# Masked self-attention with a residual: small count groups move from a shared buffer pool to spare columns of the context's bank, and one pair's turn of reciprocals changes place

## The chip, the cores and the metric

The kernel runs on one core of a Trainium2 chip. The time is device microseconds of one execution, the median of several. The figures in the profile come from one further execution that was recorded by the profiler. PE is the matrix engine, DVE the vector engine, ACT the scalar engine, POOL and SP the engines that issue most DMA transfers. PSUM is the memory that PE writes to; it has eight banks of 512 single floats per partition.

## The reference

`x` is (16, 512, 1024), batch by channel by token; `mask` is (16, 1024) of zeros and ones, about half of them ones; both weights are (512, 512).

```python
xt = jnp.transpose(x, (0, 2, 1))
q = xt @ Wq.T                                    # one projection for Q, K and V
qh = q.reshape(B, T, 8, 64).transpose(0, 2, 1, 3)
scores = scale * jnp.einsum('bhqd,bhkd->bhqk', qh, qh)
logits = (scores * cmask + (1.0 - cmask) * NEG) * rmask
attn = jax.nn.softmax(logits, axis=-1)
ctx = jnp.einsum('bhqk,bhkd->bhqd', attn, qh)
out = ctx.transpose(0, 2, 1, 3).reshape(B, T, D) @ Wo.T
return x + jnp.transpose(out, (0, 2, 1))
```

A token with mask 0 is no key, and as a query it attends to all tokens alike, so its context is the mean. Only the tokens with mask 1 need scores.

## The kernel before

**Tiling.** The sixteen batches are sorted by their number of active tokens and worked one after the other. The active tokens of a batch are gathered by indirect DMA (POOL), and up to 544 of them (528 or 512 in other batches) go through query, scores, softmax and context. The eight heads are worked as four pairs, p = 0 to 3. Each batch has 18 steps: four for each pair, and one more at 1 and at 10 for the tail tokens beyond 512.

**Who sets the order.** PE's order is written by hand: a table `plan` lists for each (step, half) which pieces of work stand there, and `free[step]` lists pieces that stand at the start of a step, ahead of its scores. Inside a batch PE does the scores of this batch (`scores`, L823), its contexts (`attend`, L858), the query projection of the next batch (`query`, L591, twelve matmuls for each half), the values (L654), and the product of the batch before with Wo (`project`, here `P_(i)`, L982, twelve matmuls, followed by the add of x on DVE, L988). The orders of DVE, ACT and SP are made by a scheduler from the program's order, ties and priorities; `high_priority(offset=HPO)` marks an instruction as urgent.

**PSUM.** `pm` hands out one of two single-bank buffers; whoever takes one waits until the reader of what stood in it is done. The other six banks are one tile, `ps` (named pss in the profile). Scores go to its banks 0 to 4 and are read there by the exps (`p<-pss`, ACT L838); the context goes to columns from 240 of banks 4 and 5. The first 240 columns of bank 5 are free, and `spot(n)` gives the first n of them. I call them the strip. All groups that use the strip use the same columns, so each waits for the reader of the group before it. Before the change the strip has four users: `index` (read by DVE at L372), `top` (L714, read by L717 into m), `bottom` (L727, read by L730 into nm) and the turn of pair 3.

**The turn.** `recip_sums` makes the reciprocal of each softmax row's sum in a column (ending in DVE L905). `recip_rows(b, p)`, the turn, transposes that column tile by one PE instruction (L912, 128x128), copies ten rows out (L917, rr), and sends them by SP to DRAM and back to all partitions (rd, rb), where `norm` multiplies the context with them (L964). Pairs 0, 1 and 2 turn in pm, pair 3 in the strip.

**Counts.** For a group of batches, `slots` works out where each active token goes: 16 matmuls with 2 to 32 columns (L254, L256, L259) give running counts `pr` and totals `pn`, read on DVE at L260, L262 and L266. It runs in batches b = 0, 2, 6, 9 and 12. `facts_end` (b = 1, 3, 7, 10 and 13) sums mask values by one matmul (L351) into `pe`, read at L352. Ahead of slots stand `permute` and `active` (DVE only), ahead of facts_end `facts_sums` (DVE only).

**Tail batches.** In b = 2, 5, 8, 11 and 14 a further product with Wo (`project_tail`) stands at step 10.

**Ties.** The framework orders accesses to one tile. `other_banks(i, ...)` declares that instruction i has nothing to do with others; `left` holds the exps in flight, `spot_reads` the reads of the strip that the next scores need not wait for.

Of the kernel before, what the change touches and what calls it, by code (L numbers as in the profile page):

```python
# [19 lines left out]
P = 128  # L20
# [27 lines left out]
class Fast:  # L48
# [12 lines left out]
    def __init__(self, ctx, tc, x, x_nat, mask_t, wq_t, wo_t, out):  # L61
        self.tc, self.nc = tc, tc.nc
        self.x, self.x_nat, self.out = x, x_nat, out
        self.B = B = x.shape[0] // T
        self.wide = [512 if b in (0, B - 2, B - 1) else C if b < 5 else 528 for b in range(B)]
        self.kept = [C if b < B - 2 else 512 for b in range(B)]
        pool = lambda name, bufs, **k: ctx.enter_context(tc.tile_pool(name=name, bufs=bufs, **k))
        self.const = pool("const", 1)
        self.one = pool("one", 1)
        self.dram = pool("dram", 8, space=bass.MemoryType.DRAM)  # L70
        self.ps_m = pool("ps_m", 2, space=PS)
        self.begun = ExitStack()
        self.ps_0 = self.begun.enter_context(tc.tile_pool(name="ps_0", bufs=2, space=PS))
        self.ps_w = self.begun.enter_context(tc.tile_pool(name="ps_w", bufs=1, space=PS))
        self.context_out, self.left, self.read, self.spots, self.spot_reads = None, [], [], False, []
# [168 lines left out]
    def slots(self, b0, b1):  # L244
# [7 lines left out]
        mb, mh = self.act  # L252
        pr = self.pm([P, B, TB])
        nc.tensor.matmul(pr, lhsT=self.tri, rhs=mh, start=True, stop=False)  # L254
        for s in range(1, TB):
            nc.tensor.matmul(pr[:, :, s:], lhsT=self.on16, rhs=mh[:, :, :TB - s], start=False, stop=(s == TB - 1))  # L256
        pn = self.pm([P, B])
        for j in range(TB):
            self.pe = nc.tensor.matmul(pn, lhsT=self.on16, rhs=mh[:, :, j], start=(j == 0), stop=(j == TB - 1)).ins  # L259
        nc.vector.tensor_copy(n, pn)  # L260
        base = self.sb([P, B, TB], F32, "sc", 3)
        nc.vector.tensor_tensor(base, self.tok.unsqueeze(1).broadcast_to([P, B, TB]), pr, ALU.subtract)  # L262
        nc.vector.tensor_tensor(base, base, n.unsqueeze(2).broadcast_to([P, B, TB]), ALU.add)
        slot = self.sb([P, NC], F32, "sc", 3)
        s3 = slot.rearrange("p (b j) -> p b j", j=TB)
        nc.vector.tensor_tensor(s3, pr, base, ALU.subtract)  # L266
        nc.vector.tensor_tensor(s3, s3, mb, ALU.mult)
# [77 lines left out]
    def facts_end(self, b0, b1):  # L345
        nc = self.nc
        B = b1 - b0
        ok = self.ok[:, b0:b1]
        t = self.sb([P, B], F32, "sc", 3)
        pe = self.pm([P, B])  # L350
        nc.tensor.matmul(pe, lhsT=self.on16, rhs=self.whole_masks, start=True, stop=True)  # L351
        nc.vector.tensor_scalar(t, pe, float(T), None, ALU.is_equal)  # L352
        nc.vector.tensor_tensor(ok, ok, t, ALU.mult)
# [9 lines left out]
    def index(self, b):  # L363
# [7 lines left out]
        base = self.base[:, b:b + 1]  # L371
        i = s["at"] = nc.vector.tensor_scalar(s["idx"], pi, base, None, ALU.add).ins  # L372
        self.spot_reads += [i] * self.spots
        with self.behind(i):
# [39 lines left out]
    def spotted(self, i):  # L414
        if self.spots:
            self.other_banks(i.ins, *self.left)
        return i

    def needs(self, i, *others):
# [290 lines left out]
    def top(self, b, g):  # L710
# [5 lines left out]
        with self.tc.high_priority(offset=HPO):  # L716
            i = nc.vector.tensor_reduce(m, pt, AX.X, ALU.max).ins  # L717
        if self.spots:
            self.other_banks(i, *self.left)
            self.spot_reads.append(i)  # L720

    def bottom(self, b, g):
# [6 lines left out]
        with self.tc.high_priority(offset=HPO):  # L729
            self.spot_reads += [nc.vector.tensor_scalar(nm[:, :HG], pb, -SCALE, None, ALU.mult).ins] * self.spots  # L730
        t = self.sb([P, HG], F32, "nq", 2)
# [56 lines left out]
    def scores(self, b, p, u):  # L788
# [46 lines left out]
        for j in (0, 1, 2, 3) if opening else (3, 0, 1, 2):  # L835
            k, i, at = places[j]
            t = self.sb([P, C], F32, "p", 12)[:, :A]
            e = nc.scalar.activation(t, flat[:, at:at + A], AF.Exp, bias=s["nm"][p // 2][:, p % 2 * 2 + k:p % 2 * 2 + k + 1],  # L838
                                     scale=SCALE, accum_out=s["z"][:, 2 * p + k, i:i + 1]).ins
            self.exp = [e]  # L840
            self.left.append(e)
# [3 lines left out]
    def attend(self, b, p, after=None):  # L845
# [18 lines left out]
        self.pend = b, p, pav, exps  # L864
        self.spot_reads = []

# [40 lines left out]
    def recip_rows(self, b, p):  # L907
# [8 lines left out]
        with self.tc.high_priority(offset=HPO):  # L916
            self.recip = nc.vector.tensor_copy(rr, pt[:10]).ins  # L917
            self.spot_reads += [self.recip] * spot
        rd = self.dram.tile([10, P], F32, tag="rd", name="rd")
# [174 lines left out]
    def run(self, flag):  # L1094
# [128 lines left out]
        if True:  # L1223
            stack = ExitStack()
            for b in range(B + 1):
# [21 lines left out]
                pk, tp, bt = ((lambda o, g, f=f, c=c: [(c, L(f, o, g))]) for f, c in ((self.peaks, 0), (self.top, 0.1), (self.bottom, 0.1)))  # L1247
                new = [g for g in groups if b == g[0] - 2], [g for g in groups if b == g[0] - 1]
                if n < B:
                    q, x, v = (lambda e, g: query(n, e, g)), xt(n), (lambda e: [(0.25, L(self.value, n, e))])  # L1250
# [7 lines left out]
                    if b:  # L1258
# [12 lines left out]
                    else:  # L1271
# [48 lines left out]
                for st, (p, i) in enumerate(S):  # L1320
# [173 lines left out]
```

## Time and profile before

| | |
|---|---|
| Time, median of 3 runs | 963.98 us (963.57 to 964.73) |
| Profiled execution, its own time | 965.21 us |
| Profiled execution, span | 963.5 us |
| PE clock granted | 0.999 of full speed |
| POOL busy | 305.1 us, 32% of the span |

The profile's page lists busy time by engine, the chain of waits that ended last, and the costliest groups. In a row of the timeline stand the start in us, the duration in us, the engine, the line, the operation, the tiles as output<-inputs, the shape, the count of instructions, and in brackets the idle time before it with what ended it. A row with a count above 1 covers that many instructions, one behind the other.

### The profile page before, as it was taken

What the parts mean: (1) busy time and instruction counts of PE and PEld (TensorE: products, weight loads), DVE (VectorE), ACT (ScalarE), POOL (GpSimd) and SP (SyncE); (2) the same over time, 40 slices, a digit from 0 to 9 for tenths busy, and PEclk for the clock granted to TensorE, in tenths of its full rate; (3) what the DMA queues carried; (4) which work ended last, traced back from release to release, by engine and by line L of the source; (5) the groups of instructions that cost most, each with busy time, mean ns of one, the idle gap of its engine ahead of it and who ended that gap; (6) DMA issues with size and microseconds to landing.
All of it is one profiled execution on the core that took longest, in us unless ns stands there. A gap on an engine that the chain in (4) does not pass through costs nothing.

```text
span 963.5 us, 22790 instructions
## 1 busy us (share of the span) xinstructions
PE 931.5 (97%) x8121; PEld 581.3 (60%) x8121; DVE 721.1 (75%) x2443; ACT 644.7 (67%) x1669; POOL 305.1 (32%) x311
## 2 busy tenths in 40 slices
PE   6799999999999999999999999999999999999997
PEld 4556656566666666666666566666666666565543
DVE  7779677776777767887678687877877788685563
ACT  4778766667677666776767678665767866665651
POOL 2102022142241513415144250522515135252452
PEclk9999999999999999999999999999999999999999
DMA  5756556556675666756656787654767757555552
GB/s 172 222 175 203 155 154 183 163 180 190 180 209 148 194 197 193 220 157 199 177 181 204 198 239 223 177 158 136 214 168 233 243 144 207 151 161 161 171 175 102
DMA packets 78568, 176.30 MB, mean 183 GB/s; under 512 B 14480, under 2 KB 22416, under 8 KB 78448
## 3 DMA queue, kind: packets, MB, share of 16 engines
q1 hardware_dynamic: 57392, 107.09, 39.8%
q0 software_dynamic: 21056, 67.68, 22.4%
q8 instruction: 66, 1.08, 0.5%
q14 instruction: 54, 0.44, 0.2%
HBM read 91.36 MB, written 33.91 MB: 130 GB/s over the span
## 4 chain that ended last, share of the span: by engine, by line
PE 81%; DVE 10%; ACT 4%; DMA 2%; issue 2%; SPq 1%; POOL 0%; POOLq 0%; DVEq 0%; ACTq 0%
PE pss L858 22%; PE pss L823 17%; PE pm L982 17%; PE pm L591 16%; ACT p L838 2%; PE pss L876 2%; PE pm L562 2%; DMA xx<-hl 1%; PE pss L766 1%; PE pm L654 1%; DVE xl L521 1%; PE pss L982 1%; DVE xa L988 1%; PE pm L912 1%; DVE p L777 1%
## 5 line engine op out<-in xcount | busy, mean ns | idle before, releaser
L838 ACT ACTIVATE p<-pss,nm 128x528 f32<-128x528 f32 (+2 forms) x512 | 353.9, 702 | 104.7 <-PE pss L823 101.5
L858 PE MATMUL pss<-p,v 128*64 128x264 f32 (+2 forms) x2048 | 242.4, 389 | 0.0
L823 PE MATMUL pss<-xx 128*128 128x118 f16 (+17 forms) x1856 | 213.6, 287 | 3.9 <-ACT p L838 2.8
L1051 POOL DMA_INDIRECT y_out<-xa,idx x68 | 82.0, 1206 | 405.2 <-DVE nq L732 85.1
L858 PEld LDWEIGHTS pss<-p,v 128*64 128x64 f32 x2048 | 141.4, 137 | 85.8 <-issue 4.9
L823 PEld LDWEIGHTS <-xx 128*128 128x128 f16 (+1 forms) x1856 | 103.2, 96 | 85.1 <-issue 34.3
L591 PE MATMUL pm<-xh,wqh 128*128 128x264 f16 (+5 forms) x512 | 141.8, 277 | 3.3 <-DVE xl L521 1.3
L591 PE MATMUL pm<-xh,wql 128*128 128x264 f16 (+5 forms) x512 | 141.1, 275 | 0.0
L591 PE MATMUL pm<-xl,wqh 128*128 128x264 f16 (+5 forms) x512 | 140.9, 275 | 0.0
L591 PEld LDWEIGHTS <-wqh 128*128 128x128 f16 x1024 | 96.4, 97 | 31.6 <-issue 12.6
L458 POOL DMA_INDIRECT xa<-x_in,idx x68 | 72.5, 1066 | 123.4 <-DMA y_out<-xa,idx 49.1
L838 ACT ACTIVATION_READ_ACCUMULATOR p<-pss,nm 128x1 f32 x512 | 105.2, 205 | 0.0
L982 PE MATMUL pm<-woh,ch 128*128 128x512 f16 x240 | 91.1, 380 | 0.0
L982 PE MATMUL pm<-woh,cl 128*128 128x512 f16 x240 | 90.9, 379 | 0.0
L982 PE MATMUL pm<-wol,ch 128*128 128x512 f16 x240 | 90.9, 379 | 0.0
L595 ACT ACTIVATE q<-pm 128x264 f32<-128x264 f32 (+5 forms) x128 | 50.8, 397 | 43.1 <-PE pm L591 42.7
L988 DVE SCALAR_TENSOR_TENSOR xa<-pm,xa 128x512 f32<-128x512 f32 x61 | 41.6, 681 | 46.0 <-PE pm L982 45.7
L1051 POOL DMA_INDIRECT y_out<-xi,idx x60 | 64.9, 1081 | 33.9 <-PE pss L766 13.4
L658 ACT COPY v<-pm 128x512 f32<-128x512 f32 x64 | 37.5, 586 | 56.0 <-PE pm L654 54.3
L982 PEld LDWEIGHTS <-ch 128*128 128x128 f16 x480 | 44.9, 98 | 47.5 <-issue 4.1
L458 POOL DMA_INDIRECT xi<-x_in,idx x60 | 59.4, 990 | 21.6 <-issue 15.8
L881 ACT COPY c<-pss 128x528 f32<-128x528 f32 (+2 forms) x64 | 38.3, 598 | 37.9 <-PE pss L876 26.8
(249 smaller groups left out, 1485.0 us busy)
## 6 DMA issues: line engine op xcount, KB each, us to landing
xm<-x_nat_in SPq DMA_DIRECT2D x60, 512.0 KB
xx<-hl SPq DMA_DIRECT2D x208, 136.0 KB
rb<-rd SPq DMA_DIRECT2D x72, 132.0 KB
xx<-hl SPq DMA_DIRECT2D x48, 128.0 KB
pt<-c SPq DMA_DIRECT2D x36, 132.0 KB
pt<-p SPq DMA_DIRECT2D x36, 132.0 KB
rb<-rd SPq DMA_DIRECT2D x32, 136.0 KB
ub<-ud SPq DMA_DIRECT2D x16, 256.0 KB
```

Source lines behind the costliest of these rows:

```text
L458: dma = self.nc.gpsimd.indirect_dma_start(out=tile[:n], out_offset=None, in_=self.x, in_offset=bass.IndirectOffsetOnAxis(ap=idx, axis=0))
L562: self.pe = nc.tensor.transpose(pt[:, c, :], x[:n, c * P:(c + 1) * P], self.ident[:n, :n]).ins
L591: self.beat = nc.tensor.matmul(pq, lhsT=w[:, c, e * P:(e + 1) * P], rhs=xx[:, c, cols], start=(k == 0), stop=(k == 3 * DC - 1)).ins
L595: nc.scalar.activation(s["q"][:, e, cols], pq, AF.Copy, scale=1.0 / (SX * SW))
L658: nc.scalar.copy(v, pv)
L823: m = nc.tensor.matmul(flat[:, c0:c1], lhsT=w, rhs=x, start=banks[n] not in banks[:n], stop=banks[n] not in banks[n + 1:])
L838: e = nc.scalar.activation(t, flat[:, at:at + A], AF.Exp, bias=s["nm"][p // 2][:, p % 2 * 2 + k:p % 2 * 2 + k + 1], scale=SCALE, accum_out ...
L858: mm = nc.tensor.matmul(pav[k * DK:(k + 1) * DK, g], lhsT=s["v"][p][:, i, k * DK:(k + 1) * DK], rhs=ps[k, i][:, cols], start=(i == 3), sto ...
L881: self.context_out = nc.scalar.copy(c[:, :A].rearrange("p (g c) -> p g c", g=2), pav).ins
L982: mm = nc.tensor.matmul(po[:cols.stop - cols.start], lhsT=a[:, e, cols], rhs=w[:, e, :], start=(e == 0 and k == 0), stop=(e == DC - 1 and ...
L988: return self.nc.vector.scalar_tensor_tensor(x, po, 1.0 / (SX * SW), x, ALU.mult, ALU.add).ins
L1051: dma = self.nc.gpsimd.indirect_dma_start(out=self.out, out_offset=bass.IndirectOffsetOnAxis(ap=idx, axis=0), in_=x, in_offset=None)
```

## The change

Three things are edited.

1. `slots` and `facts_end` take the strip in place of pm; their DVE reads are marked urgent. `slots` and `facts_sums` move from (6, 0) to (7, 1), behind query half q(1, 1); in b = 0 `slots` moves from (9, 1) to (8, 1), behind q(1, 0), and `permute` and `active` from (8, 1) to (7, 0).
2. The turn of pair 1 moves from the start of step 10, ahead of that step's other work, to behind q(2, 0) in (10, 0); in b = 0 to behind q(1, 1) in (11, 0). It stays in pm. The last batch keeps the old place.
3. A helper `seen` declares the DVE reads of the strip and the exps in flight to be independent of each other, in both directions (bottom's read in one direction only).

```diff
-        pr = self.pm([P, B, TB])
-        nc.tensor.matmul(pr, lhsT=self.tri, rhs=mh, start=True, stop=False)
+        spot = self.spot(NC + B)
+        pr, pn = spot[:, :NC].rearrange("p (b j) -> p b j", j=TB), spot[:, NC:]
+        self.spotted(nc.tensor.matmul(pr, lhsT=self.tri, rhs=mh, start=True, stop=False))
...
-        pn = self.pm([P, B])
...
-        nc.vector.tensor_copy(n, pn)
...
+        with self.tc.high_priority(offset=HPO):
+            reads = [nc.vector.tensor_copy(n, pn),
+                     nc.vector.tensor_tensor(base, self.tok.unsqueeze(1).broadcast_to([P, B, TB]), pr, ALU.subtract),
+                     nc.vector.tensor_tensor(base, base, n.unsqueeze(2).broadcast_to([P, B, TB]), ALU.add),
+                     nc.vector.tensor_tensor(s3, pr, base, ALU.subtract)]
+        self.seen(*(reads[k] for k in (0, 1, 3)))
...
-        pe = self.pm([P, B])
+        pe = self.spot(B)
...
+        with self.tc.high_priority(offset=HPO):
+            self.seen(nc.vector.tensor_scalar(t, pe, float(T), None, ALU.is_equal))
...
+    def seen(self, *reads, free=True):
+        if self.spots:
+            for i in reads:
+                self.other_banks(i.ins, *self.left)
+                self.spot_reads.append(i.ins)
+                self.free_reads += [i.ins] * free
...
+            self.seen(nc.vector.tensor_reduce(m, pt, AX.X, ALU.max))
...
+            self.seen(nc.vector.tensor_scalar(nm[:, :HG], pb, -SCALE, None, ALU.mult), free=False)
...
+            self.other_banks(e, *self.free_reads)
...
+                turn = [(0.1, L(self.recip_rows, b, 1))]
...
-                                (5, 1): vt(b, 1) + pk(b, 1), (6, 0): post,
-                                (7, 0): third + q(1, 0) + tp(b, 1), (7, 1): q(1, 1) + P_(0) + bt(b, 1), (8, 0): tc(0) + v(0) + end + rng[:2],
-                                (10, 0): tv(0) + tail + q(2, 0), (11, 0): hot + rng[2:] + early,
+                                (5, 1): vt(b, 1) + pk(b, 1),
+                                (7, 0): third + q(1, 0) + tp(b, 1), (7, 1): q(1, 1) + post + P_(0) + bt(b, 1), (8, 0): tc(0) + v(0) + end + rng[:2],
+                                (10, 0): tv(0) + tail + q(2, 0) + turn, (11, 0): hot + rng[2:] + early,
...
-                                (7, 0): tp(b, 1) + q(0, 0) + bt(b, 1) + q(0, 1), (8, 1): pre + q(1, 0),
-                                (9, 1): post, (11, 0): hot + q(1, 1),
+                                (7, 0): pre + tp(b, 1) + q(0, 0) + bt(b, 1) + q(0, 1), (8, 1): q(1, 0) + post,
+                                (11, 0): hot + q(1, 1) + turn,
...
-                            free.setdefault(st + 2, []).append(L(self.recip_rows, b, p))
+                            if p != 1 or n == B:
+                                free.setdefault(st + 2, []).append(L(self.recip_rows, b, p))
```

In the table, `tp` is top, `bt` bottom, `pk` peaks (DVE only), `tc` and `tv` the tail's copy and value, `v` a value, `rng` range checks (DVE only), `hot` and `index` the gather's indices, `end` facts_end, `post` slots or facts_sums, `pre` permute and active.

More of the change, by code (lines that the diff above doesn't have):

```diff
@@ L74, in __init__ @@
         self.ps_w = self.begun.enter_context(tc.tile_pool(name="ps_w", bufs=1, space=PS))
-        self.context_out, self.left, self.read, self.spots, self.spot_reads = None, [], [], False, []
+        self.context_out, self.left, self.read, self.spots, self.spot_reads, self.free_reads = None, [], [], False, [], []
         self.main = lambda: pool("ps_s", 1, space=PS).tile([P, 6, 512], F32, tag="s", name="pss")
@@ L252, in slots @@
         mb, mh = self.act
-        pr = self.pm([P, B, TB])
-        nc.tensor.matmul(pr, lhsT=self.tri, rhs=mh, start=True, stop=False)
+        spot = self.spot(NC + B)
+        pr, pn = spot[:, :NC].rearrange("p (b j) -> p b j", j=TB), spot[:, NC:]
+        self.spotted(nc.tensor.matmul(pr, lhsT=self.tri, rhs=mh, start=True, stop=False))
         for s in range(1, TB):
-            nc.tensor.matmul(pr[:, :, s:], lhsT=self.on16, rhs=mh[:, :, :TB - s], start=False, stop=(s == TB - 1))
-        pn = self.pm([P, B])
+            self.spotted(nc.tensor.matmul(pr[:, :, s:], lhsT=self.on16, rhs=mh[:, :, :TB - s], start=False, stop=(s == TB - 1)))
         for j in range(TB):
-            self.pe = nc.tensor.matmul(pn, lhsT=self.on16, rhs=mh[:, :, j], start=(j == 0), stop=(j == TB - 1)).ins
-        nc.vector.tensor_copy(n, pn)
+            self.pe = self.spotted(nc.tensor.matmul(pn, lhsT=self.on16, rhs=mh[:, :, j], start=(j == 0), stop=(j == TB - 1))).ins
         base = self.sb([P, B, TB], F32, "sc", 3)
-        nc.vector.tensor_tensor(base, self.tok.unsqueeze(1).broadcast_to([P, B, TB]), pr, ALU.subtract)
-        nc.vector.tensor_tensor(base, base, n.unsqueeze(2).broadcast_to([P, B, TB]), ALU.add)
         slot = self.sb([P, NC], F32, "sc", 3)
         s3 = slot.rearrange("p (b j) -> p b j", j=TB)
-        nc.vector.tensor_tensor(s3, pr, base, ALU.subtract)
+        with self.tc.high_priority(offset=HPO):
[4 more added lines that the diff above has]
+        self.seen(*(reads[k] for k in (0, 1, 3)))
         nc.vector.tensor_tensor(s3, s3, mb, ALU.mult)
@@ L349, in facts_end @@
         t = self.sb([P, B], F32, "sc", 3)
-        pe = self.pm([P, B])
-        nc.tensor.matmul(pe, lhsT=self.on16, rhs=self.whole_masks, start=True, stop=True)
-        nc.vector.tensor_scalar(t, pe, float(T), None, ALU.is_equal)
+        pe = self.spot(B)
+        self.spotted(nc.tensor.matmul(pe, lhsT=self.on16, rhs=self.whole_masks, start=True, stop=True))
+        with self.tc.high_priority(offset=HPO):
+            self.seen(nc.vector.tensor_scalar(t, pe, float(T), None, ALU.is_equal))
         nc.vector.tensor_tensor(ok, ok, t, ALU.mult)
@@ L371, in index @@
         base = self.base[:, b:b + 1]
-        i = s["at"] = nc.vector.tensor_scalar(s["idx"], pi, base, None, ALU.add).ins
-        self.spot_reads += [i] * self.spots
+        i = nc.vector.tensor_scalar(s["idx"], pi, base, None, ALU.add)
+        self.seen(i)
+        i = s["at"] = i.ins
         with self.behind(i):
@@ L716, in top @@
         with self.tc.high_priority(offset=HPO):
[L717 to L720, printed above, removed]
+            self.seen(nc.vector.tensor_reduce(m, pt, AX.X, ALU.max))
     def bottom(self, b, g):
@@ L729, in bottom @@
         with self.tc.high_priority(offset=HPO):
-            self.spot_reads += [nc.vector.tensor_scalar(nm[:, :HG], pb, -SCALE, None, ALU.mult).ins] * self.spots
+            self.seen(nc.vector.tensor_scalar(nm[:, :HG], pb, -SCALE, None, ALU.mult), free=False)
         t = self.sb([P, HG], F32, "nq", 2)
@@ L864, in attend @@
         self.pend = b, p, pav, exps
-        self.spot_reads = []
+        self.spot_reads, self.free_reads = [], []
     def attend_tail(self):
@@ L916, in recip_rows @@
         with self.tc.high_priority(offset=HPO):
-            self.recip = nc.vector.tensor_copy(rr, pt[:10]).ins
-            self.spot_reads += [self.recip] * spot
+            i = nc.vector.tensor_copy(rr, pt[:10])
+            self.seen(*[i] * spot)
+            self.recip = i.ins
         rd = self.dram.tile([10, P], F32, tag="rd", name="rd")
```

## The prediction

> **What bounds the kernel.** I read the page first (engine shares, chain), then the waits of PE, then the timeline around each place that the diff touches, and last, for the built changed program, on which earlier instruction each instruction waits.
>
> ```profile
> span 963.5 us, 22790 instructions
> PE 931.5 (97%) x8121; PEld 581.3 (60%) x8121; DVE 721.1 (75%) x2443; ACT 644.7 (67%) x1669; POOL 305.1 (32%) x311
> PE 81%; DVE 10%; ACT 4%; DMA 2%; issue 2%; SPq 1%; POOL 0%; POOLq 0%; DVEq 0%; ACTq 0%
> ```
>
> PE sets the time: it is busy for 97% of the span and carries 81% of the chain. The change adds and removes no matmul, so it can only move PE's waits. These are the ones near it (us in total, times, longest):
>
> ```profile
> PE pm L912 <- DVE rcol L905: 2.3, 3, 1.2
> PE pm L351 <- DVE xa L988: 2.1, 5, 0.4
> PE pm L254 <- DVE tmp L683: 1.6, 4, 0.4
> PE pm L591 <- DVE xl L521: 1.3, 3, 0.7
> PE pm L591 <- DVE rr L917: 1.1, 7, 0.2
> PE pm L982 <- DVE rr L917: 0.6, 4, 0.2
> ```
>
> L254 is the first matmul of slots, L351 that of facts_end, L912 the turn, L591 a query, L982 a product with Wo. One reading rule is needed below. A shown gap runs from the modelled end of a matmul, but PE issues the next one 0.1 to 0.16 us before that end (L823 at 882.81 below, with L591 until 882.97). A wait that goes is thus worth what is shown and some 0.1 to 0.16 more.
>
> **Slots move to the strip (gain).**
>
> ```profile
> 163.77 0.42 DVE L683 TENSOR_TENSOR tmp<-pm,par 128x256 f32<-128x256 f32 x1 [1.54 <-PE pm L680]
> 164.24 0.18 PE L254 MATMUL pm<-act,tri 128*128 128x32 f16 x1 [0.41 <-DVE tmp L683]
> 164.44 0.35 PE L259 MATMUL pm<-act,on 128*128 128x4 f16 x8
> ...
> 816.09 0.28 DVE L717 TENSOR_REDUCE m<-pss 128x1 f32<-128x128 f32 x1
> 816.36 0.38 PE L982 MATMUL pm<-woh,ch 128*128 128x512 f16 x1
> 816.57 0.38 PE L982 MATMUL pm<-wol,ch 128*128 128x512 f16 x1
> ```
>
> Slots takes a pm buffer that L683 still reads, in four batches (1.6 us shown in all). In the strip it waits only for the strip's last reader, m L717. Top stays ahead of q(1,1), and in these rows of a batch without slots m ends at 816.37 where the work behind q(1,1) started at 816.36: slots waits 0 to 0.03. Gain 4 x (0.41 + 0.1) = **2.04 us**. What is late next is bottom (L727), which must wait for the third read of slots (L266); between them lie the twelve matmuls of P_(0) at a pitch of 0.21, 2.5 us. If that cover failed, bottom would stall (second rival). The moved matmuls take 0.55 us before and after (164.24 to the end of L259): no change.
>
> **The turn of pair 1 goes behind the query (gain).**
>
> ```profile
> 117.48 0.38 PE L680 MATMUL pm<-ident,qt 128*128 128x128 f32 x2
> 117.68 0.28 DVE L917 COPY rr<-pm 10x128 f32<-10x128 f32 x1 [5.17 <-PE pm L912]
> 118.01 0.28 PE L591 MATMUL pm<-xh,wqh 128*128 128x272 f16 x1
> ```
>
> Before, the query needs the turn's pm buffer and stands until rr is copied: 0.15 shown and 0.16 more, 0.31. It occurs in eight batches without a tail product. Behind the query, the turn uses a buffer whose reader L683 is long done. I count seven batches (in b=1 DVE is late anyway soon after): 7 x 0.31 = **2.17 us**. Bounds: 7 x 0.15 = 1.05 and 8 x 0.31 = 2.5. The turn also moves rd and both rb transfers on SP, past at most the two pt and a ud or ub:
>
> ```profile
> 119.65 1.18 SPq L784 DMA_DIRECT2D pt<-p  x2
> 130.67 0.71 DVE L964 TENSOR_TENSOR c<-c,rb 128x544 f32<-128x544 f32 x1
> ```
>
> Their reader comes 12.7 us after the copy (117.96 to 130.67). The query's twelve matmuls at 0.11 and three transfers at some 1.2 take 5 of these: hidden, 0.
>
> **The same move in tail batches (loss).** There a product with Wo stands between the transposes and the query, and in the built program the turn gets the query's own buffer: in b=2, 5, 8 and 11 it waits for the query's copy L595 on ACT, in b=14 for xg L988. How long that is, b=14 shows:
>
> ```profile
> 882.32 0.69 DVE L988 SCALAR_TENSOR_TENSOR xg<-pm,xg 96x512 f32<-96x512 f32 x1 [2.93 <-ACT tmp L1019]
> 882.70 0.27 PE L591 MATMUL pm<-xh,wql 128*128 128x256 f16 x1
> 882.81 1.03 PE L823 MATMUL pss<-xx 128*128 128x512 f16 x4
> 883.01 0.38 ACT L595 ACTIVATE q<-pm 128x256 f32<-128x256 f32 x1 [0.72 <-PE pm L591]
> ```
>
> PE would start the turn at 882.81 and may after 883.01 + 0.38 + 0.05 = 883.44: 0.63 lost, if ACT is free at once. Of it 0.30 comes back, since L982 no longer waits for rr (0.6 in four, plus 0.15 each). b=5, 8, 11: 3 x 0.33 = **-0.99 us**; b=2 is taken below; b=14: xg ends at 883.01 and 883.05 - 882.81 = **-0.24 us**. A fifth of a microsecond more in each place, where ACT is in an exp, is the bad end (-1.0).
>
> [...]
>
> **The mask sum of facts_end moves (no gain).**
>
> ```profile
> 109.96 0.69 DVE L988 SCALAR_TENSOR_TENSOR xa<-pm,xa 128x512 f32<-128x512 f32 x1
> 110.57 0.15 DVE L730 TENSOR_SCALAR nm<-pss 128x4 f32<-128x4 f32 x1
> 110.70 0.16 PE L351 MATMUL pm<-eh,on 128*128 128x2 f16 x1 [0.41 <-DVE xa L988]
> ```
>
> L351 waits for xa on its pm buffer, 2.1 us in five places. In the strip it must wait for the reader before it, bottom's nm L730, and DVE does that right behind the same xa: it ends at 110.72, L351 starts some 0.07 later than now. 5 x 0.07 = **-0.35 us**. The bounds are +2.1, if nm came ahead of xa, and -0.75, if another 0.15 us copy slips in.
>
> **The first batch (loss).**
>
> ```profile
> 57.61 1.56 PE L823 MATMUL pss<-xx 128*128 128x512 f16 x8
> 58.73 0.71 DVE L615 TENSOR_TENSOR hl<-q,hl 128x544 f16<-128x544 f32 x1
> 59.10 3.67 PE L858 MATMUL pss<-p,v 128*64 128x256 f32 x32
> 59.37 0.29 DVE L616 COPY hl<-hl 128x544 f16<-128x544 f16 x1
> 59.91 1.20 DVE L502 TENSOR_REDUCE ms<-xm 128x1 f32<-128x1024 f32 x1
> 63.53 0.33 PE L912 MATMUL pm<-ident,rcol 128*128 128x128 f32 x1 [0.25 <-DVE n L260]
> ```
>
> Permute and active, also moved here, issue DVE work alone. Slots moves ahead of the context of pair 1 (L858), which uses the same bank and must wait for slots' third read. DVE does that read behind L615, L616 and, in the built program's order, L502: 58.73 + 0.71 + 0.29 + 1.20 = 60.93. PE is ready at 59.10 + 0.55 = 59.65. That is 1.3 us and some 0.2 for the three reads, -1.5. Back come the 0.25 and a smaller gap on the turn and the query behind it, 0.7 with the early issue. Net **-0.8 us**; bounds +0.7 (reads at once) and -1.7.
>
> **Fewer ties and DVE's new order (gain).** Marking reads as urgent and free of the exps changes no count, only what DVE does first. Two PE waits are shortened by it. In b=6:
>
> ```profile
> 392.81 0.86 DVE L224 TENSOR_TENSOR hl<-c,given 128x384 f16<-128x384 f16 x1
> 393.70 0.15 DVE L902 TENSOR_TENSOR rcol<-zt,corr 16x1 f32<-16x1 f32 x1
> 393.88 0.55 DVE L227 TENSOR_REDUCE act<-hl 128x24 f16<-128x384 f16 x1
> 394.62 0.27 PE L591 MATMUL pm<-xh,wqh 128*128 128x266 f16 x1 [0.69 <-DVE xl L521]
> ```
>
> The new order has L521 ahead of L227 and of two L902, and behind one rr copy (0.27): 0.55 + 0.30 - 0.27 = **0.58 us**. In b=2:
>
> ```profile
> 196.13 0.66 DVE L964 TENSOR_TENSOR c<-c,rb 128x544 f32<-128x544 f32 x1
> 196.71 0.15 DVE L905 TENSOR_TENSOR rcol<-rcol,hit 128x10 f32<-128x10 f32 x1
> 196.92 0.33 PE L912 MATMUL pm<-ident,rcol 128*128 128x128 f32 x1 [1.18 <-DVE rcol L905]
> ```
>
> This is the turn of pair 2, which is not moved; but L905 comes ahead of L964: **0.7 us**, in which b=2's tail loss is taken up (0.33 less at the bad end). For both, DVE's order in the built program stands against what arrives late in the run, so the low bound is 0.
>
> **Sum.** 2.04 + 2.17 + 0.58 + 0.70 = 5.49; 0.99 + 0.24 + 0.35 + 0.8 = 2.38; net 3.1 us faster. The profiled execution's own time is 965.21, so 962.1 in its terms; the median 963.98 lies 1.23 below it, so **960.9 us**.
>
> **Rivals.** *All waits go.* The diff aims at 2.1 + 1.6 + 1.1 + 0.6 + 0.25 = 5.7 us shown, and twenty-one gaps at 0.15 more make 8.8: 955.2. For it: each wait is on a pm buffer that the group no longer takes. Against it: nm stands behind the same xa, and the tail turn behind L595. *The strip's readers line up (slower).* DVE is in order, and a read of slots that stands behind queued DVE work holds bottom, as in b=0 it holds the context. If in b=2, 6, 9 and 12 L266 ends later than 2.5 us after slots' last matmul, by the 1.3 us of b=0, that is 4 x 1.3 = 5.2: 960.9 + 5.2 = 966.1. It decides for slower from a lateness of 1.26 each (3.1 + 1.9 over four). For it: DVE is 75% busy, with steps of 0.7. Against: the reads are now urgent, and the cover is 2.5. *Nothing net.* The b=6 and b=2 terms don't appear (-1.3), the rr waits give only what is shown (7 x 0.16 = 1.1 less), and b=2's tail loss counts (-0.3): 3.1 - 2.7 = 0.4 faster, 963.6.
>
> **Chances.** Forecast 0.52, with a range of its own of 958.9 to 962.6; all waits go 0.10; nothing net 0.20; slower 0.18. A measurement of this kernel can tell 0.2% (1.93 us) from no change. Faster: 0.10 and 0.47 of the forecast, 0.57; same: its other 0.05, the 0.20 and 0.01 of the slower case, 0.26; slower 0.17. The range 957.0 to 965.8 leaves out the first rival and half of the slower one, 0.19.
>
> **What would show it.** Right: no wait of slots on tmp; no query waits for rr; four new waits of the turn on q L595 of some 0.45 shown; facts_end's wait still there, now on nm, at 0.4 to 0.5; in b=0 the context waits some 1.3 us for slots' read; the waits on xl L521 and rcol L905 fall by 0.6 and 0.7. Wrong: facts_end without a wait (faster by 2), bottom waiting for slots' read (slower), the turn waiting for L595 in all batches (9 x 0.63 = 5.7 slower), or PE busy longer than 931.5 us.

## The result

| | before | changed |
|---|---|---|
| Median of 10 runs each | 964.36 us (963.39 to 966.53) | 962.04 us (959.75 to 963.10) |
| Ratio, 95% interval | | 0.9970 (0.9959 to 0.9981) |
| Profiled execution, own time | 965.21 us | 962.12 us |
| Profiled execution, span | 963.5 us | 960.4 us |

The change makes the kernel 2.3 us faster by the medians. The ratio is formed from the single runs and is not the quotient of the medians (0.9976); by it the gain is 2.9 us, and its interval puts it between 1.8 and 4.0 us. The forecast was 3.1.

The page of the changed kernel, the lines that answer to those of before:

```profile
span 960.4 us, 22815 instructions
PE 931.0 (97%) x8121; PEld 581.2 (61%) x8121; DVE 720.2 (75%) x2443; ACT 644.4 (67%) x1669; POOL 304.3 (32%) x311
PE 80%; DVE 9%; ACT 5%; DMA 4%; issue 1%; SPq 0%; POOL 0%; POOLq 0%; DVEq 0%; ACTq 0%
```

PE does the same work (931.0 us against 931.5) and still sets the time. What changed is who it waits for (us in total, times, longest). Lines below the edited functions have moved: L591 is now L602, L823 L831, L858 L867, L912 L921, L351 L353.

```profile
PE pss L353 <- DVE nm L738: 2.5, 5, 0.5
PE pm L921 <- ACT q L606: 1.9, 4, 0.5
PE pm L921 <- DVE rcol L914: 1.3, 2, 1.0
PE pss L725 <- DVE smcol L719: 1.1, 1, 1.1
PE pss L867 <- DVE sc L267: 1.0, 1, 1.0
PE pm L602 <- DVE xl L532: 0.4, 2, 0.3
```

The waits of slots on tmp (1.6) and of the query on rr (1.1) have no line any more. The wait of facts_end is still there under another name, 2.5 in place of 2.1. Four turns wait for the query's copy, 1.9 in all. The waits on rcol and xl have shrunk from 2.3 to 1.3 and from 1.3 to 0.4. New and not named in the prediction is the third line from below: PE waits 1.1 us for smcol, once.

To see what each place is worth, I take the time from the first matmul of one step's scores to the first matmul of the next step's scores, which PE reaches in the same order in both kernels, and subtract before from after. The whole run then falls into 128 stretches. Most agree within 0.02 us; these do not:

| Place | forecast, us | changed, its first profile | changed, two later profiles (after2, after3 below) |
|---|---|---|---|
| slots, b=2, 6, 9, 12 | 4 x -0.51 | -0.56, -0.56, -0.58, -0.44 | -0.56 five times, -0.57 twice, -0.13 |
| rr and the query, eight batches | 7 x -0.31 | -0.32 to -0.29, eight times | -0.33 to -0.31, eight times each |
| facts_end | 5 x +0.07 | +0.07, five times | +0.07 or +0.08, four times each; the fifth holds another wait |
| tail turns, b=2, 5, 8, 11 | +0.33 | +0.39 | +0.37 to +0.39 |
| turn, b=14 | +0.24 | +0.29 | +0.29 |
| b=2, turn of pair 2 | -1.03 | -1.38 | -1.39 |
| b=6, xl | -0.58 | -0.85 | -0.31, -0.29 |
| first batch, steps 7 to 12 | +0.8 | +0.31 | +0.33 |
| b=0 from step 16, b=1 from step 0 | 0 | +0.90 and +1.37 | +0.74 and 0; -0.05 and 0 |

Some differences are left out of the table. At the start of b=9, PE waits 0.69 us for a gathered xa in the kernel before and in no later profile (-0.66 in every one); with a single profile of the kernel before, nothing tells whether that belongs to the change. The first profile also has +1.01 at the start of b=14 (b0_back has it too, after2 and after3 don't), +0.28 from step 3 of b=9 and +0.34 in b=12. And it reaches b=0 1.5 us earlier, at its very start, which is half of the 3.1 us between the two profiled spans.

### The profile page after: what moved, and what is told of

Its sections match the earlier page's. It is cut to its first block, busy times and chain, and to the rows that moved or that the text cites. A ratio compares the mean times of both kernels' runs of the same rounds, so it can differ in the third digit from the quotient of the medians.

```text
span 960.4 us, 22815 instructions
## 1 busy us (share of the span) xinstructions
PE 931.0 (97%) x8121; PEld 581.2 (61%) x8121; DVE 720.2 (75%) x2443; ACT 644.4 (67%) x1669; POOL 304.3 (32%) x311
## 4 chain that ended last, share of the span: by engine, by line
PE 80%; DVE 9%; ACT 5%; DMA 4%; issue 1%; SPq 0%; POOL 0%; POOLq 0%; DVEq 0%; ACTq 0%
PE pss L867 21%; PE pss L831 17%; PE pm L992 17%; PE pm L602 15%; ACT p L846 3%; PE pss L885 2%; DMA xx<-hl 2%; PE pm L573 2%; PE pss L774 1%; PE pm L665 1%; DVE xl L532 1%; ACT xm L506 1%; PE pss L992 1%; PE pm L921 1%; DVE p L785 1%
## 5 line engine op out<-in xcount | busy, mean ns | idle before, releaser
L867 PE MATMUL pss<-p,v 128*64 128x264 f32 (+2 forms) x2048 | 242.4, 389 | 1.0 <-DVE sc L267 1.0
L831 PE MATMUL pss<-xx 128*128 128x118 f16 (+17 forms) x1856 | 215.1, 289 | 4.0 <-ACT p L846 2.9
L1061 POOL DMA_INDIRECT y_out<-xa,idx x68 | 79.1, 1163 | 415.2 <-DVE nq L740 117.3
L867 PEld LDWEIGHTS pss<-p,v 128*64 128x64 f32 x2048 | 141.3, 137 | 86.9 <-issue 7.3
L831 PEld LDWEIGHTS <-xx 128*128 128x128 f16 (+1 forms) x1856 | 104.2, 97 | 86.2 <-issue 35.3
L602 PE MATMUL pm<-xh,wqh 128*128 128x264 f16 (+5 forms) x512 | 141.8, 277 | 1.3 <-DVE xl L532 0.4
L602 PE MATMUL pm<-xh,wql 128*128 128x264 f16 (+5 forms) x512 | 141.1, 276 | 0.0
L602 PE MATMUL pm<-xl,wqh 128*128 128x264 f16 (+5 forms) x512 | 141.0, 275 | 0.0
L602 PEld LDWEIGHTS <-wqh 128*128 128x128 f16 x1024 | 96.4, 97 | 28.2 <-issue 9.4
L606 ACT ACTIVATE q<-pm 128x264 f32<-128x264 f32 (+5 forms) x128 | 50.7, 396 | 42.4 <-PE pm L602 40.9
L890 ACT COPY c<-pss 128x528 f32<-128x528 f32 (+2 forms) x64 | 38.3, 598 | 38.0 <-PE pss L885 26.7
```

Source lines behind the costliest of these rows:

```text
L602: self.beat = nc.tensor.matmul(pq, lhsT=w[:, c, e * P:(e + 1) * P], rhs=xx[:, c, cols], start=(k == 0), stop=(k == 3 * DC - 1)).ins
L606: nc.scalar.activation(s["q"][:, e, cols], pq, AF.Copy, scale=1.0 / (SX * SW))
L831: m = nc.tensor.matmul(flat[:, c0:c1], lhsT=w, rhs=x, start=banks[n] not in banks[:n], stop=banks[n] not in banks[n + 1:])
L867: mm = nc.tensor.matmul(pav[k * DK:(k + 1) * DK, g], lhsT=s["v"][p][:, i, k * DK:(k + 1) * DK], rhs=ps[k, i][:, cols], start=(i == 3), sto ...
L890: self.context_out = nc.scalar.copy(c[:, :A].rearrange("p (g c) -> p g c", g=2), pav).ins
L1061: dma = self.nc.gpsimd.indirect_dma_start(out=self.out, out_offset=bass.IndirectOffsetOnAxis(ap=idx, axis=0), in_=x, in_offset=None)
```

## The experiments

They ran on three chips on which the kernel before is slower than in the first result: it takes a median of 977.5, 978.6 and 980.7 us, and single runs lie up to 9 us off, so that the medians tell a few us apart at best. The stretches above suffer less: most places of the change repeat within 0.02 us on every chip. I give both. The kernel before was profiled once, for the first result, so all stretches are taken against that profile. Where the ratio and the quotient of the medians differ, "slower than before" and the like go by the ratio; an interval that holds 1 tells no difference.

| Kernel | median, us | before, same chip | ratio, 95% interval |
|---|---|---|---|
| b0_back | 978.24 | 977.51 | 1.0016 (0.9989 to 1.0042) |
| turn_strip | 981.43 | 977.51 | 1.0046 (1.0022 to 1.0070) |
| turn_old | 974.40 | 977.51 | 0.9971 (0.9947 to 0.9995) |
| ties_back | 980.31 | 977.51 | 1.0020 (0.9993 to 1.0046) |
| after2 (the changed kernel) | 975.33 | 978.62 | 0.9981 (0.9958 to 1.0005) |
| b0_pm | 973.72 | 978.62 | 0.9961 (0.9942 to 0.9980) |
| b0_fill | 975.84 | 978.62 | 0.9974 (0.9953 to 0.9996) |
| best2 | 979.21 | 978.62 | 1.0017 (0.9997 to 1.0038) |
| after3 (the changed kernel) | 976.40 | 980.72 | 0.9981 (0.9952 to 1.0010) |
| best3 | 973.51 | 980.72 | 0.9946 (0.9921 to 0.9970) |

**turn_old: the turn back at its old place.**

```diff
-                                (10, 0): tv(0) + tail + q(2, 0) + turn,
+                                (10, 0): tv(0) + tail + q(2, 0),
-                            if p != 1 or n == B:
-                                free.setdefault(st + 2, []).append(L(self.recip_rows, b, p))
+                            free.setdefault(st + 2, []).append(L(self.recip_rows, b, p))
```

> The changed kernel with the turn of pair 1 back at the start of step 10; counts and mask sums stay in the strip, ties stay fewer. My theory: the rr waits of queries (7 x 0.31 = 2.2 us) come back and the tail batches' loss (3 x 0.33 + 0.24 = 1.2) goes, so it is 1 us slower than the changed kernel, 963.0, still 1.3 faster than the kernel before. Rival: the move of the turn is what brings the gain, and the time falls back to 964.4.

Its waits have rr back, and no turn waits for L606:

```profile
PE pm L602 <- DVE rr L926: 0.9, 6, 0.2
PE pm L992 <- DVE rr L926: 0.6, 4, 0.2
```

By the stretches, all eight rr places are at 0.00 and all five tail places at 0.00 or -0.01 against before, while slots keeps its -0.53 to -0.56 and facts_end its +0.07. So these two terms belong to the turn alone, and 0.15 shown stands for 0.31 in time. The move of the turn saves 8 x 0.31 = 2.5 and costs 4 x 0.39 + 0.29 = 1.9: almost nothing is left of it. The ratio to before, 0.9971, is that of the changed kernel within its interval and excludes 1, so the rival (that the turn brings the gain) falls; the 1 us that the theory put between this kernel and the changed one is less than the times can tell.

**turn_strip: the turn of pair 1 in the strip.**

```diff
-        spot = self.spots and p == 3
+        spot = self.spots and (p == 3 or p == 1 and b < self.B - 1)
```

> The changed kernel with the turn of pair 1 in the strip in place of a pm buffer. My theory: the four waits of the turn for the query's copy L606 (1.9 us shown in all, 0.48 each) go, as nothing reads the query's buffer any more, and the 0.09 for xg: 4 x 0.63 + 0.24 = 2.7 us faster at most, 959.4; what can come in their place is a wait for the strip's last reader or for the context's copy to SBUF (ACT), both of which should be done. Rival: the strip lies in the tile of the scores and contexts, and the turn then waits for that copy: no gain, 962, or a loss of some tenths in each of fourteen batches.

The waits for L606 go, and the tail places turn from +0.39 to between -0.33 and -0.31 (four times) and the one of b=14 to -0.02. But two places that stood at -0.31, in b=9 and b=12, now stand at +0.33 and +0.29, from a wait for the context's copy:

```profile
PE pss L921 <- ACT c L890: 0.8, 2, 0.4
```

In time the kernel is slower than before (1.0046), so the theory missed. The same two batches are also 1.67 and 1.82 us longer from step 16 on, where every profile without the strip's turn stays within 0.01 of before (but for 0.31 once, in ties_back). The turn now hangs on the context's copy, and this copy follows a product whose operand pt comes by DMA; that this makes those stretches longer is not shown.

**ties_back: without the looser ties.**

```diff
                 for i in reads:
-                self.other_banks(i.ins, *self.left)
+                if old:
+                    self.other_banks(i.ins, *self.left)
                 self.spot_reads.append(i.ins)
-                self.free_reads += [i.ins] * free
```

> The changed kernel without its third part: only the tie that was loose before stays loose. PE's order is the same. My theory: in the changed kernel's profile b=2's wait of the second turn for rcol and b=6's wait for xl went by DVE's new order (1.4 and 0.85 us there). If the fewer ties made that order, both waits come back and each batch's context of pair 0 waits for rr of pair 3: 1.5 to 2.5 us slower than the changed kernel, 963.5 to 964.5. Rival: the new order comes from the urgent marks and the moves alone: 962, with rr of pair 3 copied later and nobody waiting for it.

The turn of pair 2 in b=2, in the changed kernel and then in this one:

```profile
195.86 0.17 DVE L914 TENSOR_TENSOR rcol<-rcol,hit 128x10 f32<-128x10 f32 x1
195.94 0.72 DVE L974 TENSOR_TENSOR c<-c,rb 128x544 f32<-128x544 f32 x1
196.19 0.29 PE L921 MATMUL pm<-ident,rcol 128*128 128x128 f32 x1
```

```profile
200.50 0.66 DVE L974 TENSOR_TENSOR c<-c,rb 128x544 f32<-128x544 f32 x1
201.08 0.16 DVE L914 TENSOR_TENSOR rcol<-rcol,hit 128x10 f32<-128x10 f32 x1
201.29 0.14 PEld L921 LDWEIGHTS pm<-ident,rcol 128*128 128x128 f32 x1 [1.41 <-issue]
201.29 0.33 PE L921 MATMUL pm<-ident,rcol 128*128 128x128 f32 x1 [1.19 <-issue]
```

With the ties, the 0.66 us product with rb stands ahead of the 0.16 us step that PE waits for, and the gap of 1.2 us is back. The place of b=2 is at 0.00 against before, that of b=6 at 0.00 too (-0.24 to -0.28 in the three kernels beside it); the others keep what the change gave them, but for slots in b=12 (-0.35). Without the third part of the change neither gain is there; whether it would bring them without the urgent marks was not run. No context waits for rr of pair 3, so that part of the theory missed. In time the kernel is at 1.0020, against 0.9981 for the changed kernel on the two other chips: some 4 us, of which these places explain 1.6.

**b0_back: the first batch's counts behind the context again, still in the strip.**

```diff
-                                (7, 0): pre + tp(b, 1) + q(0, 0) + bt(b, 1) + q(0, 1), (8, 1): q(1, 0) + post,
-                                (11, 0): hot + q(1, 1) + turn,
+                                (7, 0): tp(b, 1) + q(0, 0) + bt(b, 1) + q(0, 1), (8, 1): pre + q(1, 0),
+                                (9, 1): post, (11, 0): hot + q(1, 1) + turn,
```

> The changed kernel with the first batch's counts put back behind the context of pair 1, as before (still in the strip); all else as changed. My theory: the context's wait for slots' third read in b=0 (0.99 us shown, about 1.5 in place) goes, and the late part of b=0 looks as in the kernel before, with a shorter gap ahead of top (0.37 shown there against 1.05 now) and no stretch of half clock behind it. Then it is 1 to 2.2 us faster than the changed kernel, some 960 to 961. Rival: the end of b=0 is set by the load of xm that DVE waits for, so PE only meets the same wait later: the context's wait goes, the gap ahead of top grows by as much, the half clock stays, and the time stays at 962.

Both theories missed. Behind the context, slots must wait for the context's copy out of the shared tile:

```profile
PE pss L255 <- ACT c L890: 1.7, 1, 1.7
```

The first batch loses 1.8 us there (+0.98, +0.38 and +0.46 in three stretches), so this says little on its end: PE comes late and finds smcol ready. It shows why the change moves slots ahead of the context when it moves it to the strip.

**after2: the changed kernel again.**

> The changed kernel again, beside the others on one chip. In its first profile PE lost 0.9 us more than before in one wait ahead of top late in b=0 (for smcol, behind a DVE reduce that waits for a load of xm) and 1.37 us in scores that ran at half clock for some 3.4 us right behind it. My theory: this follows from the change's first batch, so it is there again, and the kernel is 2 to 3 us faster than before. Rival: it depends on how early the first load of a run comes (L205 starts at 2.9 us in the profiles that have it, at 3.9 in those that do not), the kernel before has it too in early runs, and the mean gain is the 4.5 us that the places of the change add up to.

The wait for smcol is there (+0.74), and the half clock is not: the granted clock behind it is 1.00, where the first profile has 0.50. The gap before the scores is as long as in the first profile, yet the scores behind it take their usual time (0.00). So the theory held for the wait, not for what follows it; and after3, the same kernel once more, has neither (-0.05). The rival falls by other runs: L205 starts early, at 2.9 to 3.0 us, in b0_pm, best2 and best3 too, which have the first batch as before, and none of them has the wait.

**b0_pm: the first batch wholly as before, counts in pm.**

```diff
-        spot = self.spot(NC + B)
+        spot = self.spot(NC + B) if b0 > 2 else self.pm([P, NC + B])
...
-                            if p != 1 or n == B:
+                            if p != 1 or n == B or b == 0:
```

(and the plan of b0_back, with the turn out of (11, 0))

> The changed kernel with its first batch wholly as before: counts on a pm buffer behind the context of pair 1, the turn at the start of step 10. My theory: the 0.32 us that the change's first batch costs in place goes, and PE comes late enough to the end of b=0 that the wait for smcol is short and the clock stays full: 0.3 to 2.6 us faster than the changed kernel, most likely 1.5. Rival: the wait for smcol is set by when xm lands, whatever PE does before: then it is no faster than 0.3.

No wait for smcol is left; only the one for m, as before:

```profile
PE pss L735 <- DVE m L728: 0.7, 1, 0.7
```

From step 7 of b=0 to step 3 of b=1 PE takes 38.60 us, against 38.93 in the kernel before, 39.99 in after2 and 41.52 in the first profile of the changed kernel. It is 39.21 in after3. The first batch's edits thus cost 0.6 to 1.4 us, and 2.9 with the half clock (0.50 to 0.51 granted for 3.4 us). In time b0_pm is at 973.72 against 975.33 for after2, on the same chip, as the theory said; but the intervals of the two overlap, so this rests on the profiles.

**b0_fill: matmuls in the gap.**

```diff
-                                (16, 0): q(3, 1) + tp(n, 0) + take[3:], (16, 1): bt(n, 0),
+                                (16, 0): q(3, 1) + [(0, L(keep_busy, self, 5))] + tp(n, 0) + take[3:], (16, 1): bt(n, 0),
```

> The changed kernel with five matmuls of 512 columns on constants, into a pm buffer that nobody reads, ahead of the wait for smcol late in b=0 (some 1.07 us of PE work where it stood idle for 1.05). My theory: the half clock behind that wait comes from PE's idle share just before (1.05 + 0.67 of the last 3.4 us); with 0.67 alone it stays at full clock, as in the kernel before (0.37 + 0.66). The scores behind it then take 1.7 us in place of 3.1, and the kernel is 1.3 us faster than the changed kernel although PE does more. Rival: the clock falls for another reason (the load on the chip at that moment): no gain, or 0.1 to 1 us slower where the wait would have been short.

Inconclusive. The five matmuls ran, but the wait only moved from top to bottom:

```profile
PE pss L735 <- DVE m L728: 1.7, 1, 1.7
```

PE idles 1.74 us here, as much as before the half clock of the first profile, and the clock stays full (1.00 from 77.5 to 86.5), as it also does in after2 without any filling (1.00 there too). So it tells nothing of the cause of the half clock; it does show that DVE, which waits 1.72 us for xm here, sets the end of this wait, and not PE.

**best2: three edits at once** (b0_pm; turn_strip from b=1 on; facts_end on pm).

> The changed kernel with three edits: the first batch as before, the turn of pair 1 in the strip from b=1 on, and the mask sum of facts_end back on pm. My theory by the places: first batch 0.3 to 2.6 us, four tail batches 0.7 each and b=14 0.3, facts_end 5 x 0.07: 3.7 to 6 us faster than the changed kernel, some 5.5 to 8 faster than the kernel before. Rival: the strip's turn waits for the context's copy on ACT in more places than the tail saves (0.64 in two places of one run so far): about equal to the changed kernel without its first batch.

The places do what each edit did alone: first batch -0.35 against before, tail -0.33 to -0.31, facts_end 0.00. Yet the kernel is 5.5 us slower than b0_pm beside it. So theory and rival both missed. The turn's waits for the copy L890 are 2.0 us in all, and the stretches from step 16 on, which are longer on these chips in every kernel (7.8 us in b0_pm over b=1 to 12), take 14.9. The extra lies in b=9 and b=12, with 3.92 and 4.16 us, the two batches in which turn_strip was longer there too. Their rows, of b=12:

```profile
793.47 0.60 ACT L890 COPY c<-pss 128x528 f32<-128x528 f32 x1 [3.98 <-remote]
793.50 0.28 DVE L926 COPY rr<-pm 10x128 f32<-10x128 f32 x1 [1.38 <-remote]
794.12 0.60 PE L831 MATMUL pss<-xx 128*128 128x118 f16 x3 [2.35 <-issue]
```

So the loss goes with the strip's turn, in both kernels that have it; the profile names no releaser for these waits, so the path stays open.

**after3 and best3.** best3 undoes what cost time and keeps the rest: the first batch as in b0_pm, facts_end on pm, and in the tail batches the turn at its old place.

```diff
-                turn = [(0.1, L(self.recip_rows, b, 1))]
+                turn = [] if b in tails else [(0.1, L(self.recip_rows, b, 1))]
...
-                            if p != 1 or n == B:
+                            if p != 1 or n == B or b == 0 or b in tails:
```

> The changed kernel again, on a third chip and beside the next. In place it saves 3.6 us by the profiles so far (slots 4 x 0.56, rr 8 x 0.31, b=6 0.85, b=2 1.39; against facts_end 5 x 0.07, four tails 0.39 each, b=14 0.29, first batch 1.06, b=1 0.15), and 1.4 less where half clock follows the wait late in b=0. My theory: 2.2 to 3.6 us faster than the kernel before. Rival: on chips where the pt transfers come late, part of what is saved is waited for again there, and the gain is under 2 us.

> The changed kernel with what cost it time undone: the first batch as before (counts on pm behind the context, turn at the start of step 10), the turn at the start of step 10 in the tail batches too, and the mask sum of facts_end back on pm. My theory, by the places: first batch 1.4 us (2.8 where half clock followed), four tails 0.39 each, b=14 0.29 and facts_end 5 x 0.07 come off: 3.6 us faster than the changed kernel, 7.2 faster than the kernel before, with no place slower than in the kernel before by more than 0.2. Rival: PE that is earlier meets loads and transfers that are not, and half of it is waited for again: 2 us faster than the changed kernel.

after3 is 4.3 us faster than before by the medians and 1.9 by the ratio, with an interval that reaches from 4.7 us faster to 1.0 slower; it settles neither theory. best3 is clearly faster than before: 7.2 us by the medians, 5.3 by the ratio, 2.9 to 7.7 by its interval. Against the changed kernel beside it, it is 2.9 us faster by the medians, between the theory's 3.6 and the rival's 2, and the two intervals overlap, so the times don't decide between them. Its places are as the theory has them: tail batches at 0.00 or -0.01, b=14 and facts_end at 0.00, first batch -0.17, and slots and the other rr places keep their gains. It has the lowest ratio here, though b0_pm's interval reaches as low. Its mask sum waits for xa on pm as in the kernel before:

```profile
PE pm L353 <- DVE xa L998: 2.1, 5, 0.4
```

## Why the prediction was right, and where its terms were off

**Slots: right.** Forecast 0.51 each, measured 0.56. The strip was free in time, and bottom behind P_(0) waits for nothing, as the rows of b=2 show (L267 is the third read):

```profile
168.46 0.28 DVE L728 TENSOR_REDUCE m<-pss 128x1 f32<-128x128 f32 x1
169.01 0.18 PE L255 MATMUL pss<-act,tri 128*128 128x32 f16 x1
170.39 0.18 DVE L267 TENSOR_TENSOR sc<-pss,sc 128x32 f32<-128x32 f32 x1
172.02 0.28 PE L735 MATMUL pss<-ident,m 128*128 128x4 f32 x2
```

**The turn behind the query: right.** 0.31 was forecast for each place and 0.31 measured; the reading rule (a shown 0.15 hides 0.16 of early issue) held. b=1 was counted at nothing and kept its gain (-0.32, less 0.15 two stretches on). That the turn's buffer is free in time isn't certain, though: in b=9 of b0_pm the turn waits 0.43 for L694 (L683 before), and that place stands at +0.34.

**The tail batches: right in kind, small by 0.06 each.** The rows of b=2:

```profile
183.11 0.28 PE L602 MATMUL pm<-xh,wql 128*128 128x272 f16 x1
183.43 0.40 ACT L606 ACTIVATE q<-pm 128x272 f32<-128x272 f32 x1 [0.76 <-PE pm L602]
183.88 0.33 PE L921 MATMUL pm<-ident,rcol 128*128 128x128 f32 x1 [0.49 <-ACT q L606]
```

The turn starts 0.05 behind the copy's end, as estimated from b=14. Forecast for it was 0.63 lost less 0.30; +0.39 came out.

**facts_end: right.**

```profile
111.01 0.69 DVE L998 SCALAR_TENSOR_TENSOR xa<-pm,xa 128x512 f32<-128x512 f32 x1
111.62 0.15 DVE L738 TENSOR_SCALAR nm<-pss 128x4 f32<-128x4 f32 x1
111.82 0.16 PE L353 MATMUL pss<-eh,on 128*128 128x2 f16 x1 [0.48 <-DVE nm L738]
```

The mask sum left the buffer that xa holds and met nm, which DVE does behind the same xa. The wait grew by the forecast 0.07 in every place; best3, with pm, took it back.

**DVE's order: right in kind, too small.** b=2 gave 1.38 where 0.7 with its tail loss (1.03 without) was forecast, b=6 0.85 in the first profile and 0.24 to 0.32 on the other chips. ties_back shows that both need the looser ties.

**The first batch: right in kind up to step 12, and the step that failed is its end.** The context waits for slots' third read, as the prediction had it:

```profile
56.49 1.56 PE L831 MATMUL pss<-xx 128*128 128x512 f16 x8
56.60 0.73 DVE L626 TENSOR_TENSOR hl<-q,hl 128x544 f16<-128x544 f32 x1
57.39 0.29 DVE L627 COPY hl<-hl 128x544 f16<-128x544 f16 x1
57.69 1.22 DVE L513 TENSOR_REDUCE ms<-xm 128x1 f32<-128x1024 f32 x1
58.82 0.17 DVE L267 TENSOR_TENSOR sc<-pss,sc 128x16 f32<-128x16 f32 x1
59.04 2.16 PE L867 MATMUL pss<-p,v 128*64 128x256 f32 x18 [0.99 <-DVE sc L267]
```

L513 is the 1.2 us reduce that the prediction called L502. Against 1.5 lost and 0.7 regained, 1.0 shown and 0.31 net came out. The term "net -0.8" was too dear there. What it left out is what comes next. DVE runs into a load of xm that lands late:

```profile
71.00 0.38 SPq L521 DMA_DIRECT2D xm<-x_nat_in  x1
76.41 1.22 DVE L513 TENSOR_REDUCE ms<-xm 128x1 f32<-128x1024 f32 x1 [1.88 <-DMA xm<-x_nat_in]
80.52 0.15 DVE L719 TENSOR_TENSOR smcol<-smcol,sdt 128x4 f32<-128x4 f32 x1
80.73 0.33 PE L725 MATMUL pss<-ident,smcol 128*128 128x128 f32 x1 [1.05 <-DVE smcol L719]
81.73 0.43 PE L735 MATMUL pss<-ident,m 128*128 128x4 f32 x2 [0.67 <-DVE m L728]
```

DVE idles 1.88 us for xm, everything behind that reduce is late, and PE waits 1.05 for smcol where it waited 0.37. The same load and its reader in b0_pm, which starts its first scores at the same time:

```profile
70.97 0.71 SPq L521 DMA_DIRECT2D xm<-x_nat_in  x1
74.93 1.22 DVE L513 TENSOR_REDUCE ms<-xm 128x1 f32<-128x1024 f32 x1
```

There the load is issued at the same time and has landed by 74.93. So DVE doesn't come too early here; the load comes over a microsecond later. From its issue to the reduce it is 4.7 to 6.0 us in the seven profiles with the changed first batch, where DVE waits 1.1 to 2.4 us for it, and 3.9 to 4.6 in the five others, the kernel before among them, where DVE waits 0.1 or nothing. turn_old has it too, so it goes with the moved counts and not with the turn. Why the load lands later is not shown.

In five of the seven profiles with the changed first batch the stretch around it is 0.7 to 1.6 longer than before, in turn_strip 0.09 longer and in after3 0.05 shorter; with the counts behind the context again (b0_back, b0_pm, best2, best3) it is 0.17 shorter. So the whole first batch, counted against before, cost 2.6 us in the first profile, 1.1 in after2 and 0.3 in after3, where 0.8 was forecast.

**The sum.** By the first profile the terms without the end of b=0 give 2.14 + 2.45 + 0.85 + 1.38 - 0.35 - 1.56 - 0.29 - 0.31 - 0.15 = 4.2 us, and with its end (0.90 + 1.37) 1.9. The medians say 2.3, the ratio 2.9. That the forecast of 3.1 came so near is partly luck, because errors offset each other. The terms without the end of b=0 were 1.05 too low: DVE's order by 0.62 (2.23 against 0.58 + 1.03), the first batch up to step 12 by 0.49, rr by 0.28 and slots by 0.10, less 0.44 for the tails, b=14 and b=1. The end of the first batch, where I had nothing, cost 2.3 us in the first profile (2.4 and 2.8 in turn_old and ties_back, 0.7 in after2, nothing in after3).

**The rivals.** That all waits go (955.2) fell with facts_end and the tails. That the strip's readers line up did not happen: no bottom waits for slots' read in any profile with slots behind q(1, 1). Nothing net fell too: the b=6 and b=2 gains came, and rr gave 0.31 a place and not 0.15. Sharing the strip cost facts_end 0.07 a place and made the context of the first batch wait 0.99 for slots' reader, while slots itself gained 0.56 a place by going there.

## What to carry to other kernels

A group that is moved out of a buffer can meet another wait in the new place: here facts_end no longer waited 0.41 for xa and waited 0.48 for nm. Look on the reader's engine for what stands right ahead of that reader before you count a gain. Where the turn was moved behind the query that it had held up, eight places gained 0.31, and the four in which it got the query's own buffer lost 0.39: decide place by place. When work is moved, follow its engines to their next load as well: here a load that was issued at the same time (71.00 us against 70.97 in b0_pm) was read at 76.41 in place of 74.93, and what followed held up PE at 80.73, over 20 us behind the moved work.

## What the runs showed of the hardware

The windows of the changed kernel's first profile around the wait for smcol (after the stretch and its length: busy us and count of PE, PEld, DVE, ACT and POOL, then the granted PE clock, the DMA share and GB/s):

```profile
78.50:82.00 3.50, 1.77 (x14) 1.15 (x12) 3.33 (x13) 2.79 (x9) 1.25 (x2) 0.99 0.94 262
82.00:83.50 1.50, 1.50 (x16) 1.04 (x16) 1.27 (x9) 0.86 (x3) 0.60 (x1) 0.50 0.93 358
83.50:85.40 1.90, 1.90 (x13) 0.70 (x10) 1.90 (x8) 0.65 (x2) 0.00 (x0) 0.51 0.76 228
85.40:86.40 1.00, 1.00 (x10) 0.86 (x8) 1.00 (x4) 0.86 (x3) 0.00 (x0) 1.00 0.83 234
```

And of after2:

```profile
79.50:83.00 3.50, 1.72 (x14) 1.10 (x13) 3.35 (x14) 2.75 (x9) 1.29 (x2) 1.00 0.76 251
83.00:84.50 1.50, 1.50 (x23) 0.93 (x24) 1.30 (x9) 1.04 (x3) 0.62 (x1) 1.00 0.99 393
```

PE was busy for half of 3.5 us in both (1.77 and 1.72 us), and in the first it then ran at half clock for 3.4 us (0.50 and 0.51), which cost 1.37; in the second it did not (1.00). At this place the same is seen in turn_old (clock 0.51, gaps of 1.13 and 0.67) and ties_back (0.52, gaps of 1.59 and 0.73), and not in the kernel before, turn_strip, b0_back, b0_pm and best2, whose gaps there add up to 1.13 or less (clock 1.00). In b0_fill a gap of 1.74 in one piece left the clock full (1.00). Later in the run it is no different: in b=10 of b0_pm the clock was at 0.59 from 672 to 676 us, behind a gap of 2.44, in b=8 of after2 at 1.00 in the 3.5 us behind one of 2.60. So gaps of like length come with half clock in one run and with full clock in another; what makes the clock fall is not shown.

The other surprise is the chips. The same kernel before took 964.4 us with the first result and 977.5 to 980.7 on the three chips of the experiments; whether the chip makes this or what else ran there, no run tells. In the profiles from those chips the time lies mostly in two stretches of a batch, from step 16 and from step 3 on, in rows such as these of b=10 in b0_pm (4.2 us longer than before, half clock included):

```profile
671.16 0.60 ACT L890 COPY c<-pss 128x528 f32<-128x528 f32 x1 [4.07 <-remote]
671.20 0.28 DVE L926 COPY rr<-pm 10x128 f32<-10x128 f32 x1 [0.93 <-remote]
671.82 1.23 PE L831 MATMUL pss<-xx 128*128 128x118 f16 x8 [2.44 <-issue]
```

PE, ACT and DVE stand together behind the tail product of a context, whose operand pt comes by DMA; the profile names no releaser, and what is slower on these chips stays open.
